# A four-layer graph network in float32 on one core: where ready work stands in each engine's queue, and which product begins

## The chip, the cores and the metric

The kernel runs on one core of a Trainium2 chip. Its time is the device time of one execution in microseconds (us); smaller is better. The core has a matrix engine (TensorE, PE in the profile, with its weight loads as PEld), three engines for elementwise work (VectorE or DVE, ScalarE or ACT, GpSimd or POOL) and SyncE (SP), on whose queue nearly all DMA transfers are issued. Each engine executes its own instructions in the order in which they were put in its queue, and waits on semaphores for data of the others. Results of TensorE go to PSUM banks, from where the other engines take them.

## The reference

The input is x, 128 graphs of 64 nodes with 512 features (8192 tokens), and a weighted adjacency matrix of 64 x 64 for each graph; all is float32. Each of four layers normalizes x over the features, cuts negative values (h), runs a graph operation on h and adds the result to x:

```python
h = relu(layernorm(x))
# layer 0: one weight per node
w = mask * (q * (adj @ (k * mask))).sum(-1) / sqrt(512);  x += softmax(w, nodes)[..., None] * v
# layer 1: attention with a bias on q, k, v
e = adj * exp(q @ k.T);  x += (e / e.sum(-1)) @ v
# layer 2: 8 heads, scores times 2 * adj, softmax, output projection
x += softmax((q @ k.T / 8) * 2 * adj) @ v @ Wo + bo
# layer 3: a graph attention matrix applied up to twice
t = A * exp(leaky_relu(sj + si + ab));  t = t / (t.sum(-1) + 1e-12)
x += relu(h @ Wk0 + t @ (h @ Wk1) + t @ t @ (h @ Wk2) + bk sums)
```

In layers 0 and 1, q and k meet only in a product, so the kernel folds their two weight matrices into one matrix (its result is called g). Every layer then has products of h (8192 x 512) with matrices of 512 x 512: two in layers 0 and 1 (g and v), four in layer 2 (q, k, v, o), three in layer 3 (y2, y1, y0). They are most of the arithmetic.

## The kernel before

**Tiles and loops.** 32 blocks of 256 tokens (four graphs, two tiles of 128 tokens). Layers 0 and 1 run together in pairs of blocks, then layer 2 over all blocks, then layer 3 over all blocks; x goes through DRAM between these (x1, x2). In the profile, layers 0 and 1 take up to about 1066 us (61.7 us a pair), layer 2 up to about 2005 (29.1 us a block), layer 3 the rest (22.1 us a block).

**Norm and transposition.** `norm` takes statistics (L166, L167, L169), 1/std on GpSimd (L171), nmr on VectorE (L173), h on ScalarE (L178). `transposed` turns h with TensorE (L189) into hT; the first half of it is copied out by VectorE (L194), the second by ScalarE (L192).

**A product.** Each 512 x 512 product is done by `Product` in the Strassen-Winograd form: seven half-size products. Sums of the left side (S1 to S4) are formed by GpSimd in `sums` (L213 to L216), those of the weights in advance: `formed` does it at once (L87), `later` puts four differences a matrix on a list (`chores`), and `chore(n)` takes n of them from it (L98). Product 1 uses hT alone, and needs the half that VectorE copies; product 5 uses S1, which GpSimd forms from the half that ScalarE copies. The result lives in two PSUM tiles: ab (products 1, 6, 2, 7) and dc (5, 4, 3). ScalarE and VectorE keep copies after the early products (`keep_ab`: L277, L278; `keep_dc`: L285 or L289), then the late products 2, 7, 3 are added and the result leaves (`store`: L299 to L303; `store_T`: L307 to L323; `add_to`: L332 to L339). The PSUM pool ps_mm has four buffers that go round: a product's ab and dc take the two banks of the product before the last one.

**Two products beside one another.** `side_by_side` runs the early products of two Products, then the late ones. There, the early order is 1, 5, 6, 4; a product by itself runs 1, 6, 5, 4. g and v (layers 0, 1), q and k (layer 2) and y2 and y1 (layer 3) stand side by side; v and o of layer 2 and y0 of layer 3 run by themselves. `between` holds functions that put other work into the gaps.

**What sets the order.** The program is written in one order, and a scheduler of the framework then orders each engine's instructions by when they would be ready by its own estimate, so that the order in a queue can differ from that of the text. `tc.issue_after(ins)` binds what stands in its block to a place behind `ins` in the queue of the same engine; it adds no semaphore.

**Other lines.** In layer 0, `agg` (L504) multiplies and sums into w, `wd` (L511) spreads w, and TensorE sums it over the graph (sm_w, L394, in `layer0_end`); L538 adds to x. In layer 1, `hc` (L556) sums h times a vector into the bias of the exponent (be, L559), which L563 uses on ScalarE; L580 takes reciprocals in `layer1_end`. In layer 2, L896 adds a bias to x as it is loaded, L977 adds bo to x on GpSimd, L654 to L661 are the softmax. In layer 3, L776 sums h times a vector (hu), L386 multiplies with the graph matrix (po), L846 to L851 bring y0 out, and `layer3_end` finishes the block before: tz on ScalarE (L860), L862 on GpSimd, L863 on VectorE, the store of the output (L869). The next x is loaded by L58. The list of bias sums of layer 3 is L762. The mask is loaded by L142 (mcol), and scaled by L437 (msc).

Of the kernel before, what the change touches and what calls it, by code (L numbers as in the profile page):

```python
# [8 lines left out]
FP = mybir.dt.float32  # L9
AF = mybir.ActivationFunctionType  # L10
ALU = mybir.AluOpType
AX = mybir.AxisListType

P = 128
# [4 lines left out]
TT = 2  # L19
T = TT * P  # L20
F = D // 2
# [4 lines left out]
def kernel(ctx: ExitStack, tc: tile.TileContext, a: dict, out: bass.AP):  # L26
# [7 lines left out]
    nc = tc.nc  # L34
    x_d, adj_d, adjT_d = a["x"], a["adj"], a["adjT"]
    n_tok = x_d.shape[0]
    n_blk = n_tok // T
# [15 lines left out]
    def rows(b: int):  # L53
        return slice(b * T, (b + 1) * T)

    def load_x(b: int, source, stage: int):
        x = big.tile([P, TT, D], FP, tag="x", name=f"x{stage}_{b}", bufs=4)
        nc.sync.dma_start(x, tokens(source))  # L58
        return x
# [29 lines left out]
    chores = []  # L89
# [3 lines left out]
        chores.extend((w, s) for s in sums_of_weights)  # L93

    def chore(n: int = 1):
        for _ in range(min(n, len(chores))):
            w, (to, x, y) = chores.pop(0)
            nc.gpsimd.tensor_tensor(w[:, to], w[:, x], w[:, y], ALU.subtract)  # L98

    def fetched(name: str, place: int, queue):  # L100
        w = slot(place, name)
# [25 lines left out]
    def factor(ap, which: str, layer: int, queue):  # L127
# [5 lines left out]
        return w  # L133

    first = load_x(0, x_d[rows(0), :], 0), load_adjT(0, 0)
    f0 = [
        factor(a["L0_Wqk"][:, i * D : (i + 1) * D], c, 0, queue)
        for i, (c, queue) in enumerate((("q", nc.scalar), ("k", nc.sync)))
    ]
    w0v = fetched("L0_Wv", 1, nc.sync)  # L140
    mcol = const.tile([P, n_tok // P], FP, tag="mcol", name="mcol")
    nc.sync.dma_start(mcol, a["maskcol"])  # L142
    b1q, b1k, b2q, b2k = (column(n) for n in ("L1_bq", "L1_bk", "L2_bq", "L2_bk"))
    b1v = row("L1_bv")

# [51 lines left out]
    def norm_T(x, name: str):  # L197
        hs = norm(x, name)
        return hs, transposed(hs, name)

    def sums(hT, name: str, places=("S", "S")):

        A11, A12, A21, A22 = (
            hT[:, j * 2 : (j + 1) * 2, i * P : (i + 1) * P] for i in range(2) for j in range(2)
        )
        (S1, S2), (S3, S4) = (
            (s[:, 0], s[:, 1])
            for s in (
                med.tile([P, 2, 2, P], FP, tag=tag, name=f"S{i}_{name}", bufs=6 if tag == "S" else 3)
                for i, tag in enumerate(places)  # L210
            )
        )
        nc.gpsimd.tensor_tensor(S1, A21, A22, ALU.add)  # L213
        nc.gpsimd.tensor_tensor(S2, S1, A11, ALU.subtract)
        nc.gpsimd.tensor_tensor(S4, A12, S2, ALU.subtract)
        nc.gpsimd.tensor_tensor(S3, A11, A21, ALU.subtract)  # L216
        return {1: (A11, B11), 4: (A22, T4), 5: (S1, T1), 6: (S2, T2),
                2: (A12, B21), 3: (S4, B22), 7: (S3, T3)}

    class Product:  # L220
# [39 lines left out]

        def first(self, ops, w, beside: bool = False):

            self.early(ops, w, (1, 5) if beside else (1, 6))
            if not beside:
                self.keep_ab()

# [6 lines left out]
        def keep_ab(self):  # L273


            self.p1, self.u2 = self.temp("p1"), self.temp("u2")
            nc.scalar.copy(self.p1, self.a)  # L277
            nc.vector.tensor_tensor(self.u2, self.b, self.p1, ALU.add)  # L278

        def keep_dc(self, bias=None):  # L280

# [48 lines left out]
        def add_to(self, x):  # L330

            nc.gpsimd.tensor_tensor(x[:, 0, F:], self.u2, x[:, 0, F:], ALU.add)  # L332
            nc.gpsimd.tensor_tensor(x[:, 1, F:], self.p5, x[:, 1, F:], ALU.add)
            nc.vector.tensor_tensor(self.u3, self.b, self.p1, ALU.add)
            nc.gpsimd.tensor_tensor(x[:, 1, :F], self.u3, x[:, 1, :F], ALU.add)
            nc.vector.tensor_tensor(x[:, 0, F:], self.c, x[:, 0, F:], ALU.add)
            nc.vector.tensor_tensor(x[:, 0, :F], self.a, x[:, 0, :F], ALU.add)
            nc.vector.tensor_tensor(x[:, 1, :F], self.d, x[:, 1, :F], ALU.add)
            nc.gpsimd.tensor_tensor(x[:, 1, F:], self.u3, x[:, 1, F:], ALU.add)  # L339

    def side_by_side(*parts, between=()):

        between = iter(between)
        made = []
        for ops, w, bias, store, name in parts:
            p = Product(name, bias is not None)
            p.first(ops, w, len(parts) > 1)
            if not made:  # L350
                for act in next(between, ()):
                    act()
            p.second(ops, w, bias, len(parts) > 1)
            made.append(p)
        for p, (ops, w, bias, store, name) in zip(made, parts):
            for act in next(between, ()):
                act()
            p.late(ops, w)
            store(p)
        for acts in between:  # L360
            for act in acts:
                act()

    def products(uT, vT, name: str):

# [176 lines left out]
    def layer1(b: int, x, adjT, hs, hT, between):  # L542

        m1, u1, c1, d1, w1v = made1[:5]
        ops = sums(hT, f"1_{b}")
        gT = big.tile([P, K, T], FP, tag="qk", name=f"gT_{b}")
        v = big.tile([P, TT, D], FP, tag="v", name=f"v1_{b}")
        side_by_side(
            (ops, m1, u1, lambda p: p.store_T(gT, u1), f"g1_{b}"),
            (ops, w1v, None, lambda p: p.store(v), f"v1_{b}"),  # L550
            between=between,
        )
        be = small.tile([P, TT], FP, tag="be", name=f"be_{b}")
        for t in range(TT):
            hc = med.tile([P, D], FP, tag="agg", name=f"hc_{b}_{t}", bufs=2)
            nc.vector.scalar_tensor_tensor(  # L556
                hc, hs[t], 1.0, c1, ALU.mult, ALU.mult, accum_out=be[:, t : t + 1]
            )
        nc.vector.tensor_scalar(be, be, d1, None, ALU.add)  # L559
        s = products(gT, hT, f"1_{b}")  # L560
        e = small.tile([P, TT, N], FP, tag="e", name=f"e1_{b}")
        for t in range(TT):
            nc.scalar.activation(e[:, t, :], s[:, t, :], AF.Exp, bias=be[:, t : t + 1])  # L563
        nc.vector.tensor_tensor(e, e, adjT, ALU.mult)
        return v, e
# [151 lines left out]
    def setup3():  # L717
# [41 lines left out]
        for i in range(1, 3):  # L759
            bi = med.tile([P, D], FP, tag="agg", name=f"bk{i}", bufs=2)  # L760
            nc.sync.dma_start(bi, a["L3_bk"][i : i + 1, :].to_broadcast([P, D]))
            nc.gpsimd.tensor_tensor(bs, bs, bi, ALU.add)  # L762
        return us, c3, bs

    def layer3_norm(b: int, source):
# [207 lines left out]
        later(w3[i])  # L973
    for b in range(n_blk):
        x = loaded2[b][0]
        for t in range(TT):
            nc.gpsimd.tensor_tensor(x[:, t, :], x[:, t, :], made2[1], ALU.add)  # L977
        stages = iter(())
        if b == n_blk - 2:
            stages = layer3_in(0, *normed3, made_in)  # L980
            next(stages)
        if b + 1 < n_blk:
            qk, ops = layer2_in(b + 1, normed2[b + 1], [[chore], [chore]])
        else:
            parts = layer3_step(0, False)
            next(parts)
        if b == n_blk - 2:
            w3[0] = fetched("L3_Wk0", 4, nc.sync)
            later(w3[0])
# [14 lines left out]
        else:  # L1004
            next(parts)
        side_by_side(part)
        chore(4 if b == n_blk - 2 else 0)
        nc.sync.dma_start(tokens(x2[b]), x)
        if b == n_blk - 4:
            made3 = setup3()  # L1010
# [71 lines left out]
```

## Time and profile before

| | us |
|---|---|
| median of three runs (lowest to highest) | 2736.61 (2732.79 to 2737.43) |
| the profiled execution | 2732.14 |
| its span | 2730.2 |
| TensorE busy | 2667.7 (98%) |
| VectorE busy | 1704.9 (62%) |
| GpSimd busy | 1291.3 (47%) |
| ScalarE busy | 945.8 (35%) |
| granted clock of TensorE, mean | 0.995 |

The span runs from the first to the last instruction that the profiler records. A timeline line gives the start, the duration, the engine, the line of the code, the operation, what it writes and reads, how many instructions are merged in the line, and in square brackets the idle time of the engine before it with the one that ended it. A row of waits gives total us, times and the longest one. A row of a window gives for PE, PEld, DVE, ACT and POOL the busy time and the number of instructions, and then PEclk, the clock that TensorE was granted as a part of full speed.

### The profile page before, as it was taken

The page shows a single profiled execution, that of the slowest core. Times are in us where ns is not written, and L with a number is a line of the kernel's source. Part 1 is how long each engine was busy: PE and PEld are TensorE (multiplying, and loading weights), DVE is VectorE, ACT ScalarE, POOL GpSimd, SP SyncE. Part 2 cuts the span into 40 slices and gives each one's busy share as a digit, 9 for nine tenths or more (in the row PEclk, how much of TensorE's full clock was granted, in tenths as well). Part 3 has the DMA queues.
Part 4 walks back from the last instruction along what each step waited for, and adds up shares of the span by engine and source line. Part 5 has one row for each costly group of instructions (what it writes and reads, how often), then busy time and mean ns, then how long its engine had stood idle before and what let it go on. Part 6 is the DMA issues. An engine that isn't in the chain of part 4 may idle for free.

```text
span 2730.2 us, 52850 instructions
## 1 busy us (share of the span) xinstructions
PE 2667.7 (98%) x20808; PEld 2263.4 (83%) x20808; DVE 1704.9 (62%) x4386; ACT 945.8 (35%) x2292; POOL 1291.3 (47%) x1586
## 2 busy tenths in 40 slices
PE   8999999999999998999999999999999999999998
PEld 5788888888888887899999989999887777777776
DVE  3566666666666667555555555555567666666664
ACT  2333333433333332333333333333333333333332
POOL 3434343333334337456456456456454455554454
PEclk9999999999999999999999999999999999999999
DMA  4111100111111112111111111111111111111110
GB/s 144 49 39 44 34 34 34 34 35 42 42 34 46 37 44 94 37 36 38 52 36 38 51 36 38 51 37 37 48 64 50 50 51 55 55 55 50 50 49 32
DMA packets 102345, 128.49 MB, mean 47 GB/s; under 512 B 40528, under 2 KB 49744, under 8 KB 102096
## 3 DMA queue, kind: packets, MB, share of 16 engines
q1 hardware_dynamic: 101520, 124.07, 13.6%
q8 instruction: 163, 2.67, 0.4%
q10 hardware_dynamic: 576, 1.05, 0.1%
q14 instruction: 86, 0.70, 0.1%
HBM read 74.76 MB, written 50.33 MB: 46 GB/s over the span
## 4 chain that ended last, share of the span: by engine, by line
PE 71%; DVE 17%; POOL 4%; DMA 4%; ACT 2%; issue 2%; SPq 0%; ACTq 0%; POOLq 0%; DVEq 0%
PE ab_y L248 10%; PE dc_y L248 8%; PE ab_v L248 7%; PE dc_v L248 6%; PE ab_q L241 4%; PE ab_g L248 4%; PE ab_k L241 4%; PE ab_g L241 3%; PE po L386 3%; PE dc_k L241 3%; PE dc_q L241 3%; PE dc_g L248 2%; PE tr L189 2%; DMA x<-x 2%; PE dc_g L241 2%; DVE e L654 2%
## 5 line engine op out<-in xcount | busy, mean ns | idle before, releaser
L178 ACT ACTIVATE h<-x,nmr,rstd 128x512 f32<-128x512 f32 x256 | 198.0, 808 | 223.5 <-DVE nmr L173 188.9
L166 DVE BATCH_NORM_STATS2 stats<-x 128x6 f32<-128x512 f32 x256 | 166.1, 676 | 71.8 <-DMA x<-x 67.5
L171 POOL TENSOR_TENSOR rstd<-ve,neghalf 128x2 f32<-128x2 f32 x128 | 89.7, 700 | 254.6 <-DVE ve L169 254.4
L248 PE MATMUL ab_y<-L_Wk,hT 128*128 128x256 f32 x768 | 204.3, 388 | 3.3 <-DVE u_y L300 2.6
L248 PE MATMUL ab_v<-L_Wv,hT 128*128 128x256 f32 x768 | 201.9, 385 | 3.8 <-DVE u_v L278 2.9
L248 PE MATMUL dc_y<-L_Wk,S 128*128 128x256 f32 x768 | 199.8, 383 | 0.7
L248 PE MATMUL dc_v<-L_Wv,S 128*128 128x256 f32 x768 | 197.2, 379 | 1.7 <-DVE v L302 1.7
L248 PE MATMUL ab_y<-L_Wk,S 128*128 128x256 f32 x768 | 197.8, 380 | 0.0
L248 PE MATMUL ab_v<-L_Wv,S 128*128 128x256 f32 x768 | 197.1, 379 | 0.0
L248 PEld LDWEIGHTS ab_y<-L_Wk,hT 128*128 128x128 f32 x768 | 137.8, 190 | 70.1 <-issue 25.2
L248 PEld LDWEIGHTS dc_y<-L_Wk,S 128*128 128x128 f32 x768 | 144.6, 191 | 26.4 <-DVE y L850 6.9
L248 PEld LDWEIGHTS dc_v<-L_Wv,S 128*128 128x128 f32 x768 | 145.8, 190 | 21.9 <-DVE v L302 2.1
L248 PEld LDWEIGHTS ab_v<-L_Wv,S 128*128 128x128 f32 x768 | 146.1, 190 | 20.0
L862 POOL TENSOR_TENSOR tz<-tz,y 128x512 f32<-128x512 f32 x64 | 92.9, 1452 | 145.8 <-ACT tz L860 145.8
L248 PEld LDWEIGHTS ab_y<-L_Wk,S 128*128 128x128 f32 x768 | 143.8, 191 | 18.3
L248 PEld LDWEIGHTS ab_v<-L_Wv,hT 128*128 128x128 f32 x768 | 133.9, 191 | 19.1 <-DVE u_v L278 3.2
L323 POOL TENSOR_TENSOR qk<-u_q,p_q 128x256 f32<-128x256 f32 x32 | 23.3, 727 | 265.4 <-DVE u_q L307 265.4
L189 PE MATMUL tr<-ident,h 128*128 128x128 f32 x1024 | 135.8, 275 | 3.9 <-ACT h L178 2.2
L189 PEld LDWEIGHTS tr<-ident,h 128*128 128x128 f32 x1024 | 119.9, 142 | 15.7 <-ACT h L178 2.6
L278 DVE TENSOR_TENSOR u_v<-ab_v,p_v 128x256 f32<-128x256 f32 x96 | 40.6, 423 | 126.2 <-ACT p_v L277 126.2
L213 POOL TENSOR_TENSOR S<-hT 128x256 f32<-128x256 f32 x128 | 99.4, 776 | 35.5 <-ACT hT L192 33.1
L216 POOL TENSOR_TENSOR S<-hT 128x256 f32<-128x256 f32 x128 | 106.9, 835 | 1.6 <-DVE hT L194 0.4
(243 smaller groups left out, 6535.8 us busy)
## 6 DMA issues: line engine op xcount, KB each, us to landing
x<-x SPq DMA_DIRECT2D x128, 512.0 KB, 3.4
x<-in_x_dram SPq DMA_DIRECT2D x32, 512.0 KB, 3.5
out_dram<-x SPq DMA_DIRECT2D x31, 512.0 KB, 2.7
adjT<-in_adjT_dram SPq DMA_DIRECT2D x64, 64.0 KB, 2.0
adjq<-in_adj_dram SPq DMA_DIRECT2D x64, 64.0 KB, 2.3
L_Wk<-in_L_Wk_dram SPq DMA_DIRECT2D x16, 256.0 KB, 4.4
L_Wv<-in_L_Wv_dram SPq DMA_DIRECT2D x12, 256.0 KB, 4.6
q<-in_L_Wqk_dram ACTq DMA_DIRECT2D x4, 256.0 KB, 5.9
```

Source lines behind the costliest of these rows:

```text
L166: nc.vector.bn_stats(stats[:, t, :], x[:, t, :])
L171: nc.gpsimd.tensor_tensor(rstd, ve, neghalf, ALU.pow)
L178: nc.scalar.activation(h, x[:, t, :], AF.Relu, bias=nmr[:, t : t + 1], scale=rstd[:, t : t + 1])
L189: nc.tensor.transpose(pt[:, k, :], h[:, k * P : (k + 1) * P], ident)
L213: nc.gpsimd.tensor_tensor(S1, A21, A22, ALU.add)
L216: nc.gpsimd.tensor_tensor(S3, A11, A21, ALU.subtract)
L241: nc.tensor.matmul(dst[:, m * P : (m + 1) * P], w[:, place, k, m * P : (m + 1) * P], left[:, k, :], start=key not in self.begun, stop=last ...
L248: nc.tensor.matmul(dst, left[:, k, :], w[:, place, k, :], start=key not in self.begun, stop=last and k == 1, skip_group_check=True,)
L278: nc.vector.tensor_tensor(self.u2, self.b, self.p1, ALU.add)
L386: nc.tensor.matmul(ps[t][half[g ^ t]], e[half[g], t, :], us[t][half[g]], start=True, stop=True)
L654: nc.vector.tensor_tensor(eh, eh, mx.unsqueeze(2).to_broadcast([P, TT * hq, N]), ALU.subtract)
L862: nc.gpsimd.tensor_tensor(tz[t], tz[t], y0[:, t, :], ALU.add)
```

## The change

Six things move; what is computed stays the same.

- The mask's DMA is issued right after the first x and adjacency, before the weights k and v.
- `sums` and `add_to` record their last GpSimd instruction in `behind`, and `chore` puts its differences behind that one. The calls of `chore` are spread: in layer 2 one difference in each of eight blocks (two in the first), and two and two for Wk0 at the end. In the resulting GpSimd queue, the differences of layer 2's weights stand singly or in twos over pairs 1 and 2 and from layer 1 into layer 2, and one for Wk2 or Wk1 stands between L333 and L335 of each of the first eight blocks of layer 2.
- L977 (x += bo) and L762 are bound behind `behind` too; L977 stands right behind L339 of the block before.
- `hc` of layer 1 (L556) is bound behind `kept`, the L278 of the value product. In VectorE's queue it then stands behind L173 of the next norm, or about the reciprocals of L580, instead of ahead of wd.
- Side by side, the early order is 5, 1, 6, 4, in all four layers.
- On SP's queue, the second load of x2 in layer 2 stands behind the fetches of Wk2, and an adjacency of layer 3 before the loads of bk.

The number of instructions of every engine is unchanged.

```diff
--- before.py
+++ after.py
@@ -93,9 +93,10 @@
         chores.extend((w, s) for s in sums_of_weights)
 
     def chore(n: int = 1):
-        for _ in range(min(n, len(chores))):
-            w, (to, x, y) = chores.pop(0)
-            nc.gpsimd.tensor_tensor(w[:, to], w[:, x], w[:, y], ALU.subtract)
+        with tc.issue_after(behind[0].ins):
+            for _ in range(min(n, len(chores))):
+                w, (to, x, y) = chores.pop(0)
+                nc.gpsimd.tensor_tensor(w[:, to], w[:, x], w[:, y], ALU.subtract)
 
     def fetched(name: str, place: int, queue):
         w = slot(place, name)
@@ -133,13 +134,13 @@
         return w
 
     first = load_x(0, x_d[rows(0), :], 0), load_adjT(0, 0)
+    mcol = const.tile([P, n_tok // P], FP, tag="mcol", name="mcol")
+    nc.sync.dma_start(mcol, a["maskcol"])
     f0 = [
         factor(a["L0_Wqk"][:, i * D : (i + 1) * D], c, 0, queue)
         for i, (c, queue) in enumerate((("q", nc.scalar), ("k", nc.sync)))
     ]
     w0v = fetched("L0_Wv", 1, nc.sync)
-    mcol = const.tile([P, n_tok // P], FP, tag="mcol", name="mcol")
-    nc.sync.dma_start(mcol, a["maskcol"])
     b1q, b1k, b2q, b2k = (column(n) for n in ("L1_bq", "L1_bk", "L2_bq", "L2_bk"))
     b1v = row("L1_bv")
 
@@ -198,6 +199,8 @@
         hs = norm(x, name)
         return hs, transposed(hs, name)
 
+    behind = [None]
+
     def sums(hT, name: str, places=("S", "S")):
 
         A11, A12, A21, A22 = (
@@ -213,7 +216,7 @@
         nc.gpsimd.tensor_tensor(S1, A21, A22, ALU.add)
         nc.gpsimd.tensor_tensor(S2, S1, A11, ALU.subtract)
         nc.gpsimd.tensor_tensor(S4, A12, S2, ALU.subtract)
-        nc.gpsimd.tensor_tensor(S3, A11, A21, ALU.subtract)
+        behind[0] = nc.gpsimd.tensor_tensor(S3, A11, A21, ALU.subtract)
         return {1: (A11, B11), 4: (A22, T4), 5: (S1, T1), 6: (S2, T2),
                 2: (A12, B21), 3: (S4, B22), 7: (S3, T3)}
 
@@ -260,7 +263,7 @@
 
         def first(self, ops, w, beside: bool = False):
 
-            self.early(ops, w, (1, 5) if beside else (1, 6))
+            self.early(ops, w, (5, 1) if beside else (1, 6))
             if not beside:
                 self.keep_ab()
 
@@ -275,7 +278,7 @@
 
             self.p1, self.u2 = self.temp("p1"), self.temp("u2")
             nc.scalar.copy(self.p1, self.a)
-            nc.vector.tensor_tensor(self.u2, self.b, self.p1, ALU.add)
+            self.kept = nc.vector.tensor_tensor(self.u2, self.b, self.p1, ALU.add)
 
         def keep_dc(self, bias=None):
 
@@ -336,7 +339,9 @@
             nc.vector.tensor_tensor(x[:, 0, F:], self.c, x[:, 0, F:], ALU.add)
             nc.vector.tensor_tensor(x[:, 0, :F], self.a, x[:, 0, :F], ALU.add)
             nc.vector.tensor_tensor(x[:, 1, :F], self.d, x[:, 1, :F], ALU.add)
-            nc.gpsimd.tensor_tensor(x[:, 1, F:], self.u3, x[:, 1, F:], ALU.add)
+            behind[0] = nc.gpsimd.tensor_tensor(
+                x[:, 1, F:], self.u3, x[:, 1, F:], ALU.add
+            )
 
     def side_by_side(*parts, between=()):
 
@@ -360,6 +365,7 @@
         for acts in between:
             for act in acts:
                 act()
+        return made
 
     def products(uT, vT, name: str):
 
@@ -545,7 +551,7 @@
         ops = sums(hT, f"1_{b}")
         gT = big.tile([P, K, T], FP, tag="qk", name=f"gT_{b}")
         v = big.tile([P, TT, D], FP, tag="v", name=f"v1_{b}")
-        side_by_side(
+        _, of_v = side_by_side(
             (ops, m1, u1, lambda p: p.store_T(gT, u1), f"g1_{b}"),
             (ops, w1v, None, lambda p: p.store(v), f"v1_{b}"),
             between=between,
@@ -553,9 +559,10 @@
         be = small.tile([P, TT], FP, tag="be", name=f"be_{b}")
         for t in range(TT):
             hc = med.tile([P, D], FP, tag="agg", name=f"hc_{b}_{t}", bufs=2)
-            nc.vector.scalar_tensor_tensor(
-                hc, hs[t], 1.0, c1, ALU.mult, ALU.mult, accum_out=be[:, t : t + 1]
-            )
+            with tc.issue_after(of_v.kept.ins):
+                nc.vector.scalar_tensor_tensor(
+                    hc, hs[t], 1.0, c1, ALU.mult, ALU.mult, accum_out=be[:, t : t + 1]
+                )
         nc.vector.tensor_scalar(be, be, d1, None, ALU.add)
         s = products(gT, hT, f"1_{b}")
         e = small.tile([P, TT, N], FP, tag="e", name=f"e1_{b}")
@@ -759,7 +766,8 @@
         for i in range(1, 3):
             bi = med.tile([P, D], FP, tag="agg", name=f"bk{i}", bufs=2)
             nc.sync.dma_start(bi, a["L3_bk"][i : i + 1, :].to_broadcast([P, D]))
-            nc.gpsimd.tensor_tensor(bs, bs, bi, ALU.add)
+            with tc.issue_after(behind[0].ins):
+                nc.gpsimd.tensor_tensor(bs, bs, bi, ALU.add)
         return us, c3, bs
 
     def layer3_norm(b: int, source):
@@ -973,17 +981,19 @@
         later(w3[i])
     for b in range(n_blk):
         x = loaded2[b][0]
-        for t in range(TT):
-            nc.gpsimd.tensor_tensor(x[:, t, :], x[:, t, :], made2[1], ALU.add)
+        with tc.issue_after(behind[0].ins):
+            for t in range(TT):
+                nc.gpsimd.tensor_tensor(x[:, t, :], x[:, t, :], made2[1], ALU.add)
         stages = iter(())
         if b == n_blk - 2:
             stages = layer3_in(0, *normed3, made_in)
             next(stages)
         if b + 1 < n_blk:
-            qk, ops = layer2_in(b + 1, normed2[b + 1], [[chore], [chore]])
+            qk, ops = layer2_in(b + 1, normed2[b + 1], [[], [lambda: chore(1 if b else 2)]])
         else:
             parts = layer3_step(0, False)
             next(parts)
+            chore(2)
         if b == n_blk - 2:
             w3[0] = fetched("L3_Wk0", 4, nc.sync)
             later(w3[0])
@@ -1004,7 +1014,7 @@
         else:
             next(parts)
         side_by_side(part)
-        chore(4 if b == n_blk - 2 else 0)
+        chore(2 if b == n_blk - 2 else 0)
         nc.sync.dma_start(tokens(x2[b]), x)
         if b == n_blk - 4:
             made3 = setup3()
```

## The prediction

> **What bounds the kernel now.** I read the engines' shares first.
>
> ```profile
> PE 2667.7 (98%) x20808; PEld 2263.4 (83%) x20808; DVE 1704.9 (62%) x4386; ACT 945.8 (35%) x2292; POOL 1291.3 (47%) x1586
> ```
>
> TensorE is busy 2667.7 of 2730.2 us, and the change leaves the number of instructions of every engine as it is: only their order moves. So nothing can be won or lost but TensorE's waits and the stretches at half clock that follow some of them. Next I read what TensorE's instructions waited for (total us, times, longest us).
>
> ```profile
> PE sm_w L394 <- DVE wd L511: 9.8, 15, 0.7
> PE ab_g L241 <- DVE u_g L278: 7.5, 16, 4.0
> PE ab_q L241 <- DVE hT L194: 6.0, 28, 0.4
> ...
> PE tw_k L410 <- DVE q L416: 3.9, 2, 3.3
> ```
>
> Three of these recur in every pair of blocks or in every block; the fourth is the start. A wait costs more than its idle time, because the matmul behind it is slow to refill: comparing each start with the usual pace of its kind, I get 0.81 us for a wait at sm_w, 0.40 for one at ab_g, and 0.36 for one at ab_q. I use these excesses below. All sums stand against the profiled execution, 2732.1 us (span 2730.2); the median of the runs is 2736.6, and I take the same difference off it.
>
> **The start: mask first (gain 4).** VectorE holds the scaled mask in front of the evictions of q that tw_k waits for.
>
> ```profile
> 13.43 1.26 DVE L437 TENSOR_SCALAR msc<-mcol 128x64 f32<-128x64 f32 x1 [4.92 <-DMA mcol<-in_maskcol_dram]
> ...
> 15.34 3.36 PE L410 MATMUL tw_k<-ident,k 128*128 128x128 f32 x15 [3.33 <-DVE q L416]
> ```
>
> With the mask's DMA third on SP's queue instead of eleventh, msc is done before q. The wait of 3.33 goes, and with it perhaps half of the half-clock stretch after it (clock 0.55 from 15.3 to 18.6, worth some 1.5). The four transfers of k on SP's queue start one issue, 0.34 us, later. Between 2 and 5, I take 4.
>
> **Weight sums of layer 2, early (gain 6).** VectorE and GpSimd slow each other; in pair 1, POOL forms eight differences (L98) in one burst from 66 to 90, and TensorE loses 1.99 us at 88.32, 2.33 at 93.34 and 1.7 at half clock behind the second. After the change they are spread over pairs 1 and 2, two or so between others. Between 3 and 6; I take 6, as the later pairs, with none, show nothing like it.
>
> **Layer 1's hc moved behind v's kept half (gain 18.2).** It is `hc` (L556, two per block) that stands ahead of wd on VectorE:
>
> ```profile
> 900.34 1.20 DVE L556 SCALAR_TENSOR_TENSOR hc<-h,c 128x512 f32<-128x512 f32 x1
> ...
> 901.81 0.46 DVE L511 TENSOR_TENSOR wd<-eye,w 128x128 f32<-128x128 f32 x1
> ...
> 902.33 0.49 PE L394 MATMUL sm_w<-wd,ones_bd 128*128 128x128 f32 x2 [0.65 <-DVE wd L511]
> ...
> 902.86 0.68 DVE L556 SCALAR_TENSOR_TENSOR hc<-h,c 128x512 f32<-128x512 f32 x1
> ```
>
> In the new order wd follows agg (L504, ending 900.42) at once and ends at about 900.9; sm_w would like to start at 902.33 - 0.65 = 901.68. The wait is covered by 0.8 us. The second hc, 0.68, stood ahead of u_g (L278) as well: with 1.20 + 0.68 gone from its queue, u_g is ready some 1.7 before its 0.24 idle, so the wait at ab_g goes too. 15 pairs x (0.81 + 0.40) = 18.2. The hc now stand after nmr (L173) or about the reciprocal of L580, where the next user of VectorE's queue is not due for over a microsecond; were that cover missing, each pair would lose up to 1.2, which gives 0 for this part as the lower bound.
>
> **Layers 0 and 1: product 5 before product 1 (0).** Product 5 needs S1 from POOL and the dc bank. In the trace S1 is there at least 1.0 us before the first product begins and the bank at least 1.4. If cover failed, at most one product, 0.87 us, would lie behind the wait.
>
> **From layer 1 to layer 2 (gain 9).** Here bursts of POOL stand beside VectorE:
>
> ```profile
> 1030.66 3.39 DVE L538 SCALAR_TENSOR_TENSOR x<-gv,att,x 128x512 f32<-128x512 f32 x2
> 1031.79 5.83 POOL L98 TENSOR_TENSOR L_Wo<-L_Wo 128x512 f32<-128x512 f32 x4
> 1035.68 2.08 PE L241 MATMUL ab_g<-hT,fold 128*128 128x128 f32 x8 [4.00 <-DVE u_g L278]
> ```
>
> The two L538 take 3.39 us beside L98, against 1.42 elsewhere, and u_g comes 4 us late. Excesses up to 1096: 4.4 + 1.8 + 1.9 + 1.8 + 1.8 + 1.1 = 12.8, and 1.7 at half clock. The changed order takes the bursts of seven (Wv, Wo) and of eight (Wk2, Wk1) apart; two or three differences and the 2.52 us of x += bo (L977) remain nearby, and on SP's queue the load of x2_2 is now behind all of Wk2's fetches. I leave 3 to 6 of the 14.5, and take 9 (5 to 13).
>
> The Trainium skill ("GPSIMD Engine Reference", Key points) says that GpSimd shares its SBUF interfaces with VectorE, and that instructions with two SBUF inputs contend. The row above agrees (1.70 us each for 0.71), and the rule speaks against a spread: each difference still slows what it meets, only elsewhere. At the rate of the row, 8 differences of 1.26 that each double what runs beside them would give 10 us back. I don't charge that: where they go in layer 2 (next part) VectorE is idle for 1.33 us, and L977, moved to just behind L339, meets only u_q (0.42 us at 1502.57), whose bank isn't wanted until 1506.43.
>
> **Layer 2: queries begin with product 5 (gain 10.1), and the eight chores (loss 6.2).**
>
> ```profile
> 1523.77 0.72 POOL L213 TENSOR_TENSOR S<-hT 128x256 f32<-128x256 f32 x1
> 1524.85 0.68 DVE L194 COPY hT<-tr 128x512 f32<-128x512 f32 x1
> 1525.68 0.46 PE L241 MATMUL ab_q<-hT,L_Wq 128*128 128x128 f32 x2 [0.19 <-DVE hT L194]
> ```
>
> Product 1 waits for VectorE's half of hT (ends 1525.53), product 5 for S1 (ends 1524.49) and for v's dc bank (free at 1524.93): both are early by more than half a microsecond. 28 x 0.36 = 10.1.
> The keys swap too, and k's dc bank is o's, released by L338:
>
> ```profile
> 1501.46 0.73 POOL L339 TENSOR_TENSOR x<-u_o,x 128x256 f32<-128x256 f32 x1
> 1501.54 0.42 DVE L338 TENSOR_TENSOR x<-dc_o,x 128x256 f32<-128x256 f32 x1 [1.33 <-POOL x L335]
> ```
>
> L338 waits for L335 and ends at 1501.96; k's first product begins at 1502.86, and 0.36 sooner once q's wait is gone: 0.54 to spare. But in the first eight blocks a difference of 1.26 us now stands between L333 and L335 on a POOL that has no gap there, so L338 ends at 1503.22, and k waits 0.77: 8 x 0.77 = 6.2 (0, if POOL had run ahead, to 8).
>
> **From layer 2 to layer 3 (gain 2.2).** The burst for Wk0 (1991.2 to 1997.2) goes; the waits at 1996.45 (1.6) and 2004.19 (0.7) with it.
>
> **Layer 3: y1 begins with product 5 (loss 22).** This part speaks against the change. Three lines of one block (start, duration):
>
> ```profile
> 2396.79 1.03 PE L248 MATMUL ab_y<-L_Wk,hT 128*128 128x256 f32 x4
> ...
> 2397.45 0.42 DVE L850 TENSOR_TENSOR y<-dc_y,u_y 128x256 f32<-128x256 f32 x1
> ...
> 2397.92 1.13 PE L248 MATMUL dc_y<-L_Wk,S 128*128 128x256 f32 x4
> ```
>
> Six tiles a block go round four banks, so y1's dc takes the bank of y0 of the block before, which L850 releases at 2397.87. Product 1 (ab) runs meanwhile, from 2396.79, and product 5 starts 0.05 after the release. With 5 first, nothing can run from 2396.79 to 2397.92, and product 1 comes behind. The loss is the room that product 1 filled: 0.87 us where dc already waited (16 blocks), and the distance from ab's start to L850's end + 0.05 in 11 others (0.65 to 0.85, sum 8.2); in the blocks near either end L850 is early. 16 x 0.866 + 8.2 = 22.0. It is paid in every block, since L850 is the end of a loop: L386's po (2378.56), tz, L863, the store of x, the next load of x landing in that buffer, L166 at 2390.92, and VectorE without a gap to L850, 19.3 us after po. Po comes behind the stall, so a late TensorE moves the loop with it, and it never catches up.
>
> **Sum.** 4 + 6 + 18.2 + 0 + 9 + 10.1 - 6.2 + 2.2 - 22.0 = 21.3. 2732.1 - 21.3 = 2710.8 profiled, 2736.6 - 21.3 = 2715.3 as median.
>
> **Rivals.**
> First, L850 comes earlier than I think, and layer 3 doesn't stall: 2715 - 22 = 2693. Against it: VectorE's order in layer 3 is the same, and it starts when the load lands. For it: y0's bank might be released sooner in a loop with another phase, as in block 1 (0.95 us early).
> Second, the clock (slower). The Trainium skill ("TensorE: Matmul & The Clock Gate", A second HAM failure mode) reports that micro-idles between groups of matmuls, caused by cycling PSUM banks, made the clock oscillate between half and full. Layer 3 would be that: a half-clock stretch of 3.41 us per stall costs 1.7, 27 x 1.7 = 46, and 2715 + 46 = 2761. The trace (PE busy, then PEclk after ACT's and POOL's):
>
> ```profile
> 88.40:91.70 3.30, 2.78 (x12) 2.12 (x12) 1.10 (x2) 0.00 (x0) 3.30 (x4) 1.00 0.01 2
> 93.42:96.82 3.40, 3.40 (x13) 3.05 (x14) 2.43 (x5) 1.42 (x3) 1.53 (x3) 0.50 0.00 0
> ```
>
> Behind an idle time of 1.82 (88.32) the clock stayed full, behind 2.17 (93.34) it fell to half. The stalls to come are of 0.7 to 1.2, so by the rows they cost no clock. The rival decides once half the stalls gate it (13 x 1.7 = 22).
> Third, the gain in the pairs stays out: hc in its new place makes u_g or e late instead. 2715 + 18 = 2733.
> Fourth, the gains at the boundaries stay out, because each difference slows VectorE wherever it is: 2715 + 15 = 2730.
>
> **How the numbers follow.** The forecast 0.65, no stall in layer 3 0.12, the clock 0.05, the pairs 0.08, the boundaries 0.10. The likeliest case alone reaches from 2707 to 2725 by its terms (start 2, pair 1 3, boundary 4, layer 2 6). The range for 8 in 10 takes in the fourth rival and leaves out most of the first and the clock: 2699 to 2731. A measurement tells about 0.2%, 5.5 us, from no change: faster is under 2731.1, which holds the forecast, the first, and three quarters of the last: 0.65 + 0.12 + 0.08 = 0.85. Same: the third, mostly, and the rest, 0.09. Slower: the clock and a mishap of the third, 0.06.
>
> **What would show it.** In the changed kernel's waits, sm_w, ab_g L241 and ab_q L241 are gone, tw_k's is under 0.5, and a new row has dc_y L248 waiting for DVE y L850 27 times or so, for 0.7 to 1.2 each; PEclk stays at 9 there. dc_k waits for x L338 in eight blocks. A pair lasts 60.5 instead of 61.7 us, a block of layer 3 0.8 longer, a block of layer 2 0.36 shorter. It is wrong if dc_y's wait is missing, if hc makes a new wait in the pairs, or if the clock falls in layer 3.

## The result, and the profile after

The changed kernel takes 2701.6 us (median; 2698.18 to 2704.14), the kernel before beside it 2734.7: a ratio of 0.9876, 95% interval 0.986 to 0.9891. That is 33 us less, where 19 to 21 were forecast. The profiled executions differ by 33.8 in span (2730.2 to 2696.4). The shares of the engines and what TensorE waited for, after:

```profile
PE 2657.1 (99%) x20808; PEld 2266.7 (84%) x20808; DVE 1678.1 (62%) x4386; ACT 945.1 (35%) x2292; POOL 1277.1 (47%) x1586
```

```profile
PE ab_o L251 <- DVE u_o L281: 6.7, 29, 0.5
PE tw_q L416 <- DMA q<-in_L_Wqk_dram: 5.3, 3, 4.6
PE ab_v L251 <- DVE stats L167: 4.6, 3, 2.2
PE s L641 <- POOL qk L326: 3.5, 1, 3.5
...
PE pc L702 <- DVE r L842: 2.3, 1, 2.3
...
PE dc_y L251 <- DVE u_y L855: 0.6, 2, 0.4
PE tw_k L416 <- DVE q L422: 0.5, 1, 0.5
```

The waits at sm_w, at ab_g for u_g in each pair, at ab_q for hT and the long one at tw_k are gone, as forecast. Two things are not as forecast: dc_y hardly waits (0.6 in all, and not for L858, which is L850 of the kernel before), and a new row heads the list, ab_o waiting for u_o 29 times.

Both programs run the same 20808 matmuls, so I compared the start times of matmuls of the same number in the two traces, counted from the first one. The difference that builds up between such places gives each stretch its part. Stretches are in us of the kernel before; the forecast column is the prediction's terms laid onto them.

| stretch | what lies in it | forecast | measured |
|---|---|---|---|
| to 109 | start, pair 1 | -10.0 | -11.1 |
| 109 to 973 | 14 pairs of layers 0 and 1 | -16.9 | -20.7 |
| 973 to 1083 | last pair, into layer 2 | -10.2 | -10.0 |
| 1083 to 1386 | first blocks of layer 2, with eight differences | +3.0 | +8.7 |
| 1386 to 1993 | the rest of layer 2 | -6.9 | -1.4 |
| 1993 to the end | into layer 3, layer 3 | +19.8 | +1.3 |
| sum | | -21.2 | -33.2 |

Each row is one profiled execution against one. The 14 pairs gain 20.1 to 20.7 in all nine kernels here that have the change to hc; the start gains 6.7 to 11.1 in the eight kernels that share its edits, so that row is uncertain by some 4 us. The last row hides two things: 2.0 are gained from 1993 to 2010, as forecast (2.2), and 4.3 are lost from 2020 to 2040, where pc waits 2.3 for VectorE's r (1.0 before). What moved r was not tested.

The forecast fails in layers 2 and 3, and the experiments are mostly about these. Here is the same place of layer 3 as was shown of before, a block of the changed kernel:

```profile
2361.80 1.03 PE L251 MATMUL dc_y<-L_Wk,S 128*128 128x256 f32 x4
...
2361.96 0.42 DVE L856 TENSOR_TENSOR y<-dc_y,u_y 128x256 f32<-128x256 f32 x1
2362.29 0.41 DVE L858 TENSOR_TENSOR y<-dc_y,u_y 128x256 f32<-128x256 f32 x1
...
2362.76 0.30 PEld L251 LDWEIGHTS ab_y<-L_Wk,hT 128*128 128x128 f32 x2 [0.34 <-DVE y L858]
```

y1's product 5 (dc_y, from S) begins at 2361.80, while VectorE is still reading y0's dc tile until 2362.70. So it can't be writing into that bank. It is product 1, now second, that starts 0.06 after L858: what was forecast of dc holds for ab. The four banks of the pool go round as a ring. In the two built programs y0 of block 20 and y1 of block 21, the next to use its banks, have these:

```
before   y0: ab 5, dc 4     y1: ab 5, dc 4
after    y0: ab 2, dc 3     y1: ab 3, dc 2
```

In the changed program y1's dc has y0's ab bank in 30 of 31 blocks; the program in which only the order of the products is changed has the same. In all three programs, 721 of 725 tiles, taken in the order in which they are first written, get the bank whose tile before has its last use earliest. With 5 ahead of 1 the tile written first is dc, and y0's ab is used up before its dc.

And the place in layer 2 where product 5 was to save a wait of 0.36:

```profile
1490.28 0.68 DVE L195 COPY hT<-tr 128x512 f32<-128x512 f32 x1
...
1490.75 0.38 PE L244 MATMUL dc_q<-S,L_Wq 128*128 128x128 f32 x2
...
1490.88 0.41 DVE L281 TENSOR_TENSOR u_o<-ab_o,p_o 128x256 f32<-128x256 f32 x1
...
1491.35 1.13 PE L251 MATMUL ab_o<-L_Wo,cT 128*128 128x256 f32 x4 [0.22 <-DVE u_o L281]
```

Product 5's two hoisted matmuls no longer wait for hT. But behind them stand o's late products, which add into ab and so wait until u_o is taken from it, and u_o stands on VectorE right behind the copy of hT. The wait has only moved, two matmuls on.

### The profile page after: what moved, and what is told of

It is laid out like the page before. It is cut to its first block, busy times and chain, and to the rows that moved or that the text cites. A ratio compares the mean times of both kernels' runs of the same rounds, so it can differ in the third digit from the quotient of the medians.

```text
span 2696.4 us, 52807 instructions
## 1 busy us (share of the span) xinstructions
PE 2657.1 (99%) x20808; PEld 2266.7 (84%) x20808; DVE 1678.1 (62%) x4386; ACT 945.1 (35%) x2292; POOL 1277.1 (47%) x1586
## 4 chain that ended last, share of the span: by engine, by line
PE 78%; DVE 11%; DMA 5%; POOL 3%; ACT 2%; issue 1%; SPq 0%; ACTq 0%; POOLq 0%; DVEq 0%
PE ab_y L251 10%; PE ab_v L251 10%; PE dc_v L251 8%; PE dc_y L251 7%; PE ab_g L244 4%; PE ab_g L251 4%; DMA x<-x 4%; PE ab_k L244 3%; PE dc_g L244 3%; PE ab_q L244 3%; PE dc_g L251 3%; PE po L392 3%; PE tr L190 3%; PE dc_k L244 2%; PE dc_q L244 2%; DVE e L661 2%
## 5 line engine op out<-in xcount | busy, mean ns | idle before, releaser
L167 DVE BATCH_NORM_STATS2 stats<-x 128x6 f32<-128x512 f32 x256 | 167.1, 675 | 77.7 <-DMA x<-x 70.5
L251 PE MATMUL ab_y<-L_Wk,hT 128*128 128x256 f32 x768 | 206.6, 392 | 3.4 <-DVE u_y L303 2.6
L251 PE MATMUL ab_v<-L_Wv,hT 128*128 128x256 f32 x768 | 202.7, 387 | 5.0 <-DVE stats L167 4.6
L251 PEld LDWEIGHTS ab_y<-L_Wk,hT 128*128 128x128 f32 x768 | 137.0, 191 | 74.5 <-issue 25.1
L251 PE MATMUL ab_v<-L_Wv,S 128*128 128x256 f32 x768 | 198.3, 381 | 0.0
L251 PE MATMUL dc_v<-L_Wv,S 128*128 128x256 f32 x768 | 198.2, 381 | 0.0
L251 PE MATMUL ab_y<-L_Wk,S 128*128 128x256 f32 x768 | 197.9, 380 | 0.0
L251 PE MATMUL dc_y<-L_Wk,S 128*128 128x256 f32 x768 | 192.7, 380 | 0.6 <-DVE u_y L855 0.6
L251 PEld LDWEIGHTS ab_v<-L_Wv,S 128*128 128x128 f32 x768 | 147.0, 191 | 19.9
L251 PEld LDWEIGHTS dc_y<-L_Wk,S 128*128 128x128 f32 x768 | 145.8, 190 | 21.3 <-DVE u_y L855 1.7
L251 PEld LDWEIGHTS dc_v<-L_Wv,S 128*128 128x128 f32 x768 | 144.2, 191 | 19.0 <-issue 0.8
L251 PEld LDWEIGHTS ab_y<-L_Wk,S 128*128 128x128 f32 x768 | 144.4, 191 | 18.2
L251 PEld LDWEIGHTS ab_v<-L_Wv,hT 128*128 128x128 f32 x768 | 136.5, 191 | 22.5 <-ACT qk L323 6.8
```

Source lines behind the costliest of these rows:

```text
L167: nc.vector.bn_stats(stats[:, t, :], x[:, t, :])
L251: nc.tensor.matmul(dst, left[:, k, :], w[:, place, k, :], start=key not in self.begun, stop=last and k == 1, skip_group_check=True,)
```

## The experiments

Where a measured part is given without lines of a profile, it is read as in the table above, in us of the kernel before. Two theories stand against each other: the prediction's steps, and the one formed on the two readings above. In the diffs, lines are cut to what changes.

**Product 5 first, alone.** On the kernel before:

```diff
-            self.early(ops, w, (1, 5) if beside else (1, 6))
+            self.early(ops, w, (5, 1) if beside else (1, 6))
```

> The kernel before with one edit: side by side, product 5 before product 1, in all layers. The prediction's steps: layer 2 gains 10, layer 3 loses 22, so 12 slower, about 2747, with dc_y waiting for L850. The theory formed on the result: the PSUM pool gives the bank that comes free first to the tile that is written first, so y1's dc takes y0's ab bank and layer 3 loses nothing (under 3 us); in layer 2 the wait of 0.36 for hT only moves to o's late products, which wait 0.4 for u_o, so nothing is gained there: 2735, within 4 of before.

Measured: 2736.2, ratio 1.0012 (1.0005 to 1.0019). From 1083 to 1993 it is 1.1 longer, with nothing of the 10.1, and its waits show the exchange at once: the row of ab_q is gone, and in its place is

```profile
PE ab_o L248 <- DVE u_o L278: 7.6, 31, 0.5
```

From 1993 on it is 4.5 longer, not 22; kernels with the order 1, 5 (further below) are 4.2 and 4.4 longer there too, so this much can't be put down to the order. By the medians (3.6, with an interval clear of 1) the edit by itself is a small loss.

**One ring of four banks against two of two.** On the changed kernel, so that dc always follows dc; the transposes and the folding at the start take the two names in turn:

```diff
-            ab = ps_mm.tile([P, 2, F], FP, tag="mm", name=f"ab_{name}")
-            dc = ps_mm.tile([P, 2, F], FP, tag="mm", name=f"dc_{name}")
+            ab = ps_mm.tile([P, 2, F], FP, tag="ab", name=f"ab_{name}", bufs=2)
+            dc = ps_mm.tile([P, 2, F], FP, tag="dc", name=f"dc_{name}", bufs=2)
```

> The changed kernel, with ab and dc tiles in two rings of two banks instead of one of four, so that a dc tile always follows a dc tile; order of all engines unchanged but for two transposes at the start. If the changed banks are why layer 3 lost nothing: dc_y of y1 waits about 0.9 for the last read of y0's dc (L858) in some 27 blocks, layer 3 takes 22 longer, 2723, with dc_y L251 <- DVE y L858 in the waits. If L858 is early enough without that: no new wait, 2702.

Measured: 2726.6, ratio 0.9977 (0.9969 to 0.9985), 25 above the changed kernel. The order of instructions is the same but for transposes at the start, and the wait that the prediction foresaw is there, in its waits and in a block:

```profile
PE dc_y L251 <- DVE y L858: 20.3, 27, 1.3
...
PE dc_k L244 <- DVE x L341: 1.7, 8, 0.2
```

```profile
2399.94 0.41 DVE L858 TENSOR_TENSOR y<-dc_y,u_y 128x256 f32<-128x256 f32 x1
...
2400.41 1.13 PE L251 MATMUL dc_y<-L_Wk,S 128*128 128x256 f32 x4 [0.52 <-DVE y L858]
```

dc_y waits 27 times, and from 1993 on this kernel is 21.8 longer than the kernel before; the forecast had 27 blocks and 22.0 for the wait. The price, the place and the loop were right; what was wrong was which bank. This run also answers the rival of the clock: 27 waits of up to 1.3 us, and the mean granted clock of the profiled execution stays at 0.997, and over 290 us of layer 3 its window has PEclk at 1.00 (behind POOL's busy time):

```profile
2400.00:2690.00 290.00, 281.55 (x1512) 221.02 (x1513) 185.00 (x505) 91.89 (x190) 140.20 (x167) 1.00 0.13 47
```

**hc alone.** On the kernel before:

```diff
-            nc.vector.scalar_tensor_tensor(
-                hc, hs[t], 1.0, c1, ALU.mult, ALU.mult, accum_out=be[:, t : t + 1]
-            )
+            with tc.issue_after(of_v.kept.ins):
+                nc.vector.scalar_tensor_tensor(
+                    hc, hs[t], 1.0, c1, ALU.mult, ALU.mult, accum_out=be[:, t : t + 1]
+                )
```

> The kernel before with one edit: layer 1's hc bound behind v's u2. Both theories: the waits at sm_w for wd and at ab_g for u_g go, 15 x 1.2 to 16 x 1.4, so 18 to 22 faster, about 2715. A rival, that hc only moves the wait to e or to the next agg, has no change: 2735.

Measured: 2715.1, ratio 0.9936 (0.9921 to 0.9951). The rows of sm_w and of the recurring ab_g are gone. Its 14 pairs take 20.7 less, 1.48 each, which is all that the changed kernel gains there. I had 1.21. The missing 0.27 is in the matmuls that follow a late one, which I hadn't counted: matched with the kernel before, the second half of sm_w regains 0.10, the other matmuls of ab_g 0.11 and the transposes 0.05 a pair. In the changed kernel wd is done well before sm_w, which no longer waits for it, and hc stands behind nmr:

```profile
855.58 0.69 DVE L517 TENSOR_TENSOR wd<-eye,w 128x128 f32<-128x128 f32 x1
...
858.46 0.39 PE L400 MATMUL sm_w<-wd,ones_bd 128*128 128x128 f32 x2
...
878.51 0.16 DVE L174 SCALAR_TENSOR_TENSOR nmr<-mv,rstd 128x2 f32<-128x2 f32 x1 [0.49 <-POOL rstd L172]
878.59 0.68 DVE L563 SCALAR_TENSOR_TENSOR hc<-h,c 128x512 f32<-128x512 f32 x1
```

**GpSimd's part alone.** On the kernel before, all bindings and places of chore, L977 and L762; neither hc nor mask nor the order of products:

> The kernel before with GpSimd's part of the change alone: chores bound and spread, L977 and L762 bound (the order 1, 5 stays, hc and mask stay). The prediction's steps: pair 1 gains 6, the layer boundaries 11, and the eight differences in layer 2 cost nothing here, since with 1 first k's dc is not wanted early: 17 faster, 2718. The theory formed on the result: they cost 8 or 9 all the same, because each delays add_to, the store of x, the load into that buffer and with it VectorE and v's bank: 8 to 9 faster, 2726, with PE ab_v waiting for DVE or ACT in the first blocks of layer 2.

The core of its edit:

```diff
-            qk, ops = layer2_in(b + 1, normed2[b + 1], [[chore], [chore]])
+            qk, ops = layer2_in(b + 1, normed2[b + 1], [[], [lambda: chore(1 if b else 2)]])
```

Measured: 2724.9, ratio 0.9973 (0.9965 to 0.9981), 8 less. It gains 3.9 at the start and pair 1, and stands 10.9 ahead at 1125; by 1386 it has lost 4.1 of that, in the blocks with the differences, and has the row `PE ab_v L251 <- DVE stats L167` once, with 1.5 (a row of that line in the kernel before is 0.9). So the differences cost something without 5 being first, half of what I expected of them. The spread differences, L977 and L762 were not told apart here.

**Where the differences stand.** What they do is seen in the changed kernel's worst block of these. First GpSimd, SyncE and VectorE, then what TensorE did, from the timeline:

```profile
1257.86 1.29 POOL L99 TENSOR_TENSOR L_Wk<-L_Wk 128x512 f32<-128x512 f32 x1
1259.09 0.74 POOL L338 TENSOR_TENSOR x<-u_o,x 128x256 f32<-128x256 f32 x1
1259.77 0.75 POOL L342 TENSOR_TENSOR x<-u_o,x 128x256 f32<-128x256 f32 x1
...
1260.54 0.37 SPq L1018 DMA_DIRECT2D x<-x  x1
...
1265.51 0.36 SPq L58 DMA_DIRECT2D x<-x  x1
...
1269.17 1.29 DVE L904 TENSOR_TENSOR x<-x,L_bv 128x512 f32<-128x512 f32 x2 [5.46 <-DMA x<-x]
...
1272.10 1.13 PE L251 MATMUL ab_v<-L_Wv,hT 128*128 128x256 f32 x4 [2.17 <-DVE stats L167]
```

The difference (L99) pushes the last step of add_to, that the store of x, that the load into the buffer, and that L904, which stands on VectorE ahead of the steps that free q's bank for v. Here the load's issue came 4.97 after the store's, against 2.78 in the block two before; together with 1.23 for the difference it was too much. TensorE idled 2.17, and the window behind it is at less than full clock:

```profile
1272.20:1275.50 3.30, 3.30 (x11) 2.70 (x12) 2.65 (x12) 1.91 (x5) 1.45 (x3) 0.66 0.00 0
```

This block has 4.1 of the 8.7. In the other blocks with a difference the loss is 0.2 to 0.7, once 1.7, and in two of them, followed matmul by matmul, it sits at ab_v as well, which waits for ScalarE's step that frees q's bank. The late load is not the difference's work: at this block it is slow in every kernel here (3.3 to 5.0), and with no difference ahead of it, 4.79 cost 1.0 (product 5 first, alone).

The experiment, on the changed kernel: the same eight differences bound behind L342, where GpSimd has a gap of over 8 us in the block shown:

```diff
-            behind[0] = nc.gpsimd.tensor_tensor(
+            behind[0] = added[0] = nc.gpsimd.tensor_tensor(
                 x[:, 1, F:], self.u3, x[:, 1, F:], ALU.add
...
-            qk, ops = layer2_in(b + 1, normed2[b + 1], [[], [lambda: chore(1 if b else 2)]])
+            qk, ops = layer2_in(b + 1, normed2[b + 1], [[], [lambda: chore(1 if b else 2, added[0])]])
```

> The changed kernel, with layer 2's eight differences bound behind the last step of add_to (L342) instead of ahead of its third, so that they stand in GpSimd's gap after it; nothing else moves. If the differences delay the store of x and the load into its buffer, the 8.7 lost in the first blocks of layer 2 go to under 2: about 2694. If L977's new place or SyncE's order is the cause, or VectorE is slowed by them wherever they stand: 2702.

Measured: 2695.6, ratio 0.9857 (0.9842 to 0.9873). Between 1083 and 1386 it loses 1.4 instead of 8.7; with the order 1, 5 (further below) the same stretch loses 5.1 with the differences ahead of L338 and 0.9 in the gap. The intervals of the two kernels overlap, and of the 7 won in the profile all but 1.3 is lost again behind 1910, where neither edit nor order differs and where the profiles of these kernels scatter by some 6 us. So the 6 us between the medians are not certain; what is shown is the stretch that the edit touches, and of that, too, a part is the load, which came 4.24 after the store here and 4.97 there. The order on all other engines is the same in both programs, and L977 keeps its new place, so it is not the cause.

**The copy of hT behind u_o.** On the changed kernel: VectorE's copy of layer 2's hT recorded after o's early products.

```diff
-            else:
-                nc.vector.tensor_copy(ht, pt)
+            elif held is None:
+                nc.vector.tensor_copy(ht, pt)
+            else:
+                held.append((ht, pt))
...
-        side_by_side(part)
+        side_by_side(part, between=[[copied]])
```

> The changed kernel, with VectorE's copy of layer 2's hT recorded behind o's early products, so that u_o stands ahead of it on VectorE (one hoisted matmul of q goes back to its product). If u_o is late because the copy of 0.68 stands ahead of it: the wait at ab_o goes, 28 x 0.4 = 11 faster than the changed kernel, 2690. If q's product 1 then waits for hT, or u_o waits for ScalarE's p_o anyway: 2702, with the wait at ab_q or ab_o.

Measured: 2723.4, ratio 0.9953 (0.9935 to 0.9971): 22 slower, a miss. The wait at ab_o is gone, and another has come:

```profile
PE pc L704 <- ACT pT L687: 16.8, 54, 1.0
PE ab_v L253 <- DVE stats L167: 5.9, 7, 1.9
```

The scheduler reordered more than the copy. On ScalarE, one h now stands ahead of the copies of pT that TensorE waits for:

```profile
1523.08 0.81 ACT L179 ACTIVATE h<-x,nmr,rstd 128x512 f32<-128x512 f32 x1 [1.10 <-DVE nmr L174]
1523.80 1.05 ACT L687 COPY pT<-tr 128x512 f32<-128x512 f32 x2
```

**Both of these edits together.**

> The changed kernel with both edits, the differences in the gap and the later copy of hT: if the two costs are separate, they add up, 8 + 11 = 19 faster than the changed kernel, 2683; if the first is noise of the DMAs, 2690; if neither holds, 2702.

Measured: 2710.4, ratio 0.9909 (0.9892 to 0.9926): 13 better than the later copy alone, so the differences' place is worth something there too (ab_v's row shrinks to 2.1, twice), with pc's wait still at 13.3.

**Both, with h and nmr bound behind what they had overtaken.** On the last kernel (the comments are added here):

```diff
+        with behind_of(after[0]):   # the last step of k, on VectorE
             nc.vector.scalar_tensor_tensor(nmr, mv[:, :, 0], -1.0, rstd, ALU.mult, ALU.mult)
...
+            with behind_of(after[1]):   # the last copy of pT, on ScalarE
                 nc.scalar.activation(
```

> The kernel with the differences in the gap and the later copy of hT, with the activations of h bound behind the copies of pT on ScalarE, and nmr behind the last step of k on VectorE, as they stand in the changed kernel. If the later copy lost its 11 because these two moved ahead: the wait at pc for pT goes, and 11 less than with the differences in the gap alone, 2685. If the later copy itself is the cause, it stays near 2710.

Measured: 2686.1 (2682.6 to 2687.7), ratio 0.9822 (0.9809 to 0.9835). The rows of pc for pT and of the 29 waits at ab_o are both gone; one wait of ab_o of 0.9 is left. So the moved instructions were why the later copy had lost, and the copy is worth 9 to 11 us: 9.5 by the medians of this kernel and the one with the differences in the gap alone; from 1083 to 1910 this one gains 10.1 on the kernel before, where that one loses 1.0. The binding does not restore the changed kernel's order: h and nmr stand behind the right instructions, but one block later. No run has that without the later copy. But matched with the kernel of the gap, an ordinary block gains 0.38, all of it from o's late products to q's first, where the wait for u_o was (0.22), so the copy is what shows. This kernel is 15 below the changed one, and the intervals are apart.

**The order 1, 5 in the changed kernel.**

> The changed kernel with the order 1, 5 back, everything else of the change kept. If 5 first is worth nothing or costs a little, as it did on the kernel before (3.6): 2698 to 2702, with PE ab_q waiting for hT again in place of ab_o for u_o. By the prediction's steps, undoing it loses 10 in layer 2, and layer 3 has shown no loss to win back: 2712.

Measured: 2702.4, ratio 0.9882 (0.9868 to 0.9895): no different from the changed kernel. With the differences in the gap as well:

> The changed kernel with the differences in the gap and the order 1, 5 back. If both act by themselves: 6 less for the first and 0 to 3 less for the second, 2692 to 2696; if 5 first is needed by the rest: above 2700.

Measured: 2694.1, ratio 0.9854 (0.9841 to 0.9868), against 2695.6 with 5 first. So product 5 first is by itself worth nothing that can be told. By the readings above the later copy of hT needs it, since product 1 waits for that copy; no run has the later copy with the order 1, 5.

**The mask alone.** On the kernel before, the two lines of mcol moved up:

> The kernel before with one edit: the mask's DMA right after the first x and adjacency. The prediction's step: tw_k's wait of 3.3 goes with half of the slow-clock stretch behind it, 4 faster (2 to 5), 2729. From the changed kernel's start, which is 11 ahead after two pairs where GpSimd's part alone is 4 ahead: up to 7 faster, 2726. If k's later transfers take its place: 2733.

Measured: 2727.3, ratio 0.9976 (0.9969 to 0.9983), 7 less by the medians. The profiled execution is only 1.7 shorter in span. There, tw_k's wait is gone, and a smaller one stands behind it, for the eviction of k:

```profile
14.13 1.45 DVE L460 COPY bqr<-L_bq 128x512 f32<-128x512 f32 x1 [2.72 <-DMA L_bq<-in_L_bq_dram]
15.50 1.28 DVE L416 COPY k<-tw_k 128x512 f32<-128x512 f32 x2
...
16.32 4.51 PE L424 MATMUL pf<-k,q 128*128 128x512 f32 x6 [2.34 <-DVE k L416]
```

The next DMA in line, bq's, takes the mask's place at the head of VectorE's queue. That the medians show more than the profiles may be no more than scatter: the profiled execution of before is among its faster ones (2732.1, where its medians are 2732.6 to 2736.6), that of this kernel among its slower ones (2730.6, median 2727.3).

## Why the prediction was right or wrong

The direction and the range (2699 to 2731) hold, the range by luck: without the loss of 22 in layer 3 the other terms come to 2693, outside it, and only because the 10.1 of layer 2 stayed out as well is 2701.6 inside. The forecast number was 14 too high: three of its steps failed, the largest by some 20 us, and dc_y's wait did not come, which it had named as a sign of being wrong.

*Start, pair 1, into layer 2: right, the start with an uncertain size.* 10 forecast and 11.1 measured; 10.2 and 10.0. The mask works by the mechanism named, though alone it meets the next DMA. Up to 109, the mask alone gains 1.8 and GpSimd's part alone 3.9 in the profiles, less together than any kernel that has both (6.7 at least); the rest is open. With GpSimd's part alone, 7.8 is gained between 973 and 1083, so the waits there came from the order of GpSimd's work; the bursts of L98 and L977 were not tested apart.

*hc in the pairs: right, 0.27 a pair too small.* The term left out the slower matmuls behind a late one.

*Layers 0 and 1 with product 5 first, 0: right.* Alone, the order changes the 14 pairs by 0.1.

*Layer 2's queries with product 5, 10.1: wrong.* The step asked what product 5 needs, and found it early. It didn't ask what TensorE would meet next: o's late products, whose u_o stands on VectorE behind the same copy of hT. Where a wait is ended by one of a row of instructions on an in-order engine, the next user of that row takes over the wait. Once the copy was behind u_o, and h and nmr no longer ahead of what they had overtaken, the gain came.

*The eight differences, 6.2: near in sum, wrong in mechanism.* Measured were 8.7, and not at k. In the changed kernel k's product 5 begins before L341 (L338 of the kernel before) is over, by 0.32 to 0.34 in each of those blocks, without a wait:

```profile
1259.86 0.42 DVE L341 TENSOR_TENSOR x<-dc_o,x 128x256 f32<-128x256 f32 x1 [2.56 <-POOL x L338]
...
1259.95 1.06 PE L244 MATMUL dc_k<-S,L_Wk 128*128 128x128 f32 x8
```

It is the bank again. In the program before, k's dc takes o's dc bank and waits for L338, in 30 blocks; in the changed one it takes o's ab bank, which L340 releases earlier. With two rings, where it has o's dc bank again, the wait for L341 is back: 8 times, but 0.2 each where 0.77 was forecast. The price was paid at v, through the store of x and the load behind it, which the step didn't follow, and about half of it in one block where that load is slow anyway.

*From layer 2 to layer 3, 2.2: right at its place* (2.0), with the loss behind it that the term left out.

*Layer 3's 22: wrong, for the same fact.* "Y1's dc takes the bank of y0 of the block before, which L850 releases" was read off the kernel before and carried over. The order of first writes decides the bank, and the change altered that order. With the old kind of bank forced, it was 21.8. The first rival was the right one (2693 forecast, with the layer 2 step still in it), and what was said for it ("y0's bank might be released sooner") was near: it was another bank.

*The rivals.* The clock didn't oscillate in layer 3, even with the waits forced. The micro-idles named in the Trainium skill ("TensorE: Matmul & The Clock Gate", A second HAM failure mode) cost no clock here at 0.5 to 1.3 us each. That a spread difference slows VectorE as one of a burst does is not refuted: none of the eight in layer 2 has an instruction of VectorE beside it, ahead of L338 or in the gap. Where two for Wk0 do stand beside VectorE's hu, at 1986 and 1989 us of the changed kernel, they take 1.72 each, where the eight take 1.26 to 1.29.

## What to carry to other kernels

When the order of two first writes changes, look up the PSUM banks in the new program before pricing any wait on a bank. In this framework a ring with one name gave the bank that comes free first to the tile written first; here that turned two forecast waits, in layer 3 and at k, into nothing. When a wait is taken away, price the next instruction behind it on the waiting engine against the same queue, and follow every delayed last step through its store and the next load. After one move, compare the order of all engines: a scheduler moves other work as well, and a few bindings bring back what that costs.

## What the runs showed of the hardware

The time from the issue of a 512 KB store to that of the load that waits for it wasn't steady in layer 2. In most blocks it is 2.7 to 2.8 us. Which others are slow differs, but two of the 31 blocks are slow in all 13 kernels: 3.3 to 5.0 in the one shown (1260 us), 4.2 to 5.2 in the one eleven blocks on. Why these is open. A loop that has 2 us of slack at 2.78 has none left at 4.97.

The same idle time did not always halve the clock. In the kernel before, ab_y waits 2.62 us at 2054.86, and the 3.4 us behind it have PEclk 0.51; in the changed kernel the same wait ends at 2021.72, and from there to 2027 PEclk is 1.00. In the changed kernel 2.17 and 2.29 were followed by half clock (1273 and 1993 us). So these runs show that waits of up to 1.3 us cost no clock, and no fixed limit above that.
